# A decoder layer on one core: softplus moved from VectorE to ScalarE and GpSimd, and identity products put into TensorE's queue

## The chip, the cores and the metric

The kernel runs on one core of a Trainium2 chip. The metric is the device time of one execution in microseconds; lower is better. A core has TensorE (matmul, called PE in the profile, its weight loads PEld), VectorE (DVE), ScalarE (ACT), GpSimd (POOL) and SyncE (SP), which work in parallel; each takes its instructions in order, and they wait for each other by semaphores.

## The reference

The input is 8 rows of 256 tokens with 256 features, in float32. Three parts follow each other, each with a residual and a layer norm:

```
x = layernorm(x + mamba(x))              # per row
x = layernorm(x + cross_attention(x, ctx))   # per row, with a feed-forward of 1024
x = layernorm(x + experts(x))            # 160 experts, 8 per token, and one shared
```

The part that the change touches is the step size of the mamba block, with 512 inner channels and 16 states:

```
delta = softplus(dt @ dt_w + dt_b)       # [256 tokens, 512 channels] per row
h[t]  = h[t-1] * exp(delta[t] * A) + (delta[t] * u[t]) * B[t]
y[t]  = h[t] @ C[t]
```

Softplus of v is max(v, 0) + ln(1 + exp(-|v|)), with a correction for the rounding of 1 + exp(-|v|).

## The kernel before

Channels and features lie on the 128 partitions, tokens along the free side. The program has two stages.

**The rows.** Each of the 8 rows goes through a scan of 16 steps (n = 0 to 15), each for 32 channels times 16 states. A step has a product g on GpSimd (`product`, L527), four decays on ScalarE (`decays`, L535), two scans on VectorE (`scans`, L543) and one multiplication h on VectorE (`read_out`, L551); every fourth step TensorE adds four h (`summed`, L557 and L563) and one step later VectorE gates them (`gated`, L569). Beside the scan of row b run the head of row b+1 (`head`: projection, convolution, softplus, gate), the rest of row b-1 (`rest`: out projection po, attention, feed-forward, routing) and the scatters of rows done before (`scatter`, indirect DMAs on GpSimd, L855).

The order of every engine's instructions but SyncE's is written out by hand. `head`, `rest` and the lists are generators that say `yield place, kind`; `go_on` counts places, three per scan step, and puts out all that is due. So the softplus of the next row, at places 22 to 30 of `head`, stands at steps 7 to 10 of the scan, and its instructions stand in the queues between those of the scan.

The softplus in `head`: `with_bias` (ScalarE) writes v, then |v| into e; `exp_of` makes e = exp(-|v|) and delta = 1 + e (both ScalarE, L427 and L428); `rounding` makes e = (delta - 1) - e on VectorE (L432); `log_of` makes delta = ln(delta) on ScalarE between two table loads (L437); GpSimd subtracts e (L339); `step_sizes` makes delta = max(v, 0) + delta on VectorE (L442); `spread_out` multiplies by u on GpSimd (L446) and writes both to DRAM, from where they come back spread over the partitions for the next row. Row 0's own head (`first_head`) has the same steps in another form.

**The experts.** When the scan ends, the tokens go to the experts in turns of 128 pairs: `turn_x` transposes the pairs on TensorE (L1299) and VectorE copies them (L1301), `inner` (L1312) and `outer` (L1325) multiply by an expert's weights, `store` scatters the result. The first 56 turns, kind "a", are the list made before the last row is routed (`first_list`); the rest of the last two rows runs between them, so many places per turn (`between`). The turns "b" and "few" take what is left, after the routing of the last row. Then the eight results of each token are added and normed.

**TensorE's identity products.** `warm(n)` in the kernel before multiplies the identity by ones n times into `states`, and stands only in `first_head` (L456). Results are not used. PSUM banks for the rest come from a pool of two (`bank`), those of the turns from one of two per tag; a bank is handed out again when its last reader is done. `turned` (L206) transposes four blocks on TensorE and is called four times per row, for x1, the attention's probabilities, x2 and x3; in the profile they are pt_x from xn, pt_prob, pt_x from cn and pt_x from x.

Of the kernel before, what the change touches and what calls it, by code (L numbers as in the profile page):

```python
# [9 lines left out]
F32 = mybir.dt.float32  # L10
AF = mybir.ActivationFunctionType
# [3 lines left out]
P = 128  # L15
B, S, D = 8, 256, 256
KD = D // P
TT = S // P
DI = 512
KI = DI // P  # L20
# [57 lines left out]
def decoder_layer(  # L78
# [20 lines left out]
    nc = tc.nc  # L99
# [8 lines left out]
    ident = keep.tile([P, P], F32, name="ident")  # L108
# [28 lines left out]
    minus_one = keep.tile([P, 1], F32, name="minus_one")  # L137
    nc.vector.memset(minus_one, -1.0)

    turn = keep.tile([P, 2, -(-MOST // P)], I32, name="turn")  # L140
# [5 lines left out]
    ones = keep.tile([P, P], F32, name="ones")  # L146
# [6 lines left out]
    def bank(name):  # L153
        return pools["ps"].tile([P, NT], F32, tag="ps", name=name)
# [3 lines left out]
    def tables(name):  # L158

        if in_act[0] != name:  # L160
            nc.scalar.preload_act_table_set(name)  # L161
        in_act[0] = name
# [7 lines left out]
    def moments(src, name):  # L170

        n = src.shape[1]
        st = small.tile([P, n, 6], F32, tag="st", name=f"st_{name}")
        mv = small.tile([P, n, 2], F32, tag="mv", name=f"mv_{name}")
        for c in range(n):
            nc.vector.bn_stats(st[:, c, :], src[:, c, :])  # L176
        for c in range(n):
            nc.vector.bn_aggr(mv[:, c, :], st[:, c, :])  # L178
        return mv
# [18 lines left out]
    def layernorm(dst, src, name):  # L198
        normed(dst, src, moments(src, name), name)

    def turned(src, name):

        pt = bank(f"pt_{name}").rearrange("p (k t) -> p k t", k=KD)
        for k in range(KD):
            for c in range(TT):
                nc.tensor.transpose(pt[:, k, c * P : (c + 1) * P], src[:, c, k * P : (k + 1) * P], ident)  # L206
        return pt
# [6 lines left out]
    with ExitStack() as first:  # L214
# [3 lines left out]
        m2 = scan.enter_context(tc.tile_pool(name="m2", bufs=2, side="right"))  # L218
# [70 lines left out]
        states = held.tile([P, NG, S], F32, name="states")  # L289
# [9 lines left out]
        def head(b, made):  # L299

            t = made["t"] = {}

            def bank(name):
                return ps_head.tile([P, NT], F32, tag="ps_head", name=name)

            for j in range(KI // 2):
                if j:
                    yield 7, 1
                t["pj", j] = projected(bank, b, in_x, j, "pj")
                yield 7 * j + 2, 0  # L310
                tap_now(b, j, t)
                for e in range(2):
                    yield 7 * j + 3 + e, 0
                    taps_before(b, j, e, t)
            yield 12, 0
            tables(silus)
            nc.scalar.activation(t["u"], t["u"], AF.Silu)

            gate_silu(rows_made[b - 1])
            exps()  # L320
            yield 14, 1
            t["px"] = steps_b_c(bank, b, t)
            yield 16, 0
            b_c(b, t, made)
            for j in range(KI // 2):
                yield 17 + 3 * j, 1
                pd = wider(bank, b, j, t)
                yield 19 + 3 * j, 0
                for i in range(2):
                    with_bias(b, 2 * j + i, pd[:, i, :], t)  # L330
            nc.scalar.activation(t["e"], t["v"], AF.Abs)
            yield 23, 0
            part = slice(0, KI)
            exp_of(part, t)
            yield 24, 0
            rounding(part, t, nc.vector)
            log_of(part, t)
            yield 27, 0
            nc.gpsimd.tensor_sub(t["delta"], t["delta"], t["e"])  # L339
            yield 29, 0  # L340
            step_sizes(part, t)
            yield 30, 0
            spread_out(b, part, t, made, nc.gpsimd)
            for j in range(KI // 2):
                yield 32 + 3 * j, 1
                pz = projected(bank, b, in_z, j, "pz")
                yield 34 + 3 * j, 0
                gate_part(b, j, pz, t)
            if b + 1 < B:
                load_x(b + 1)  # L350
            made["sz"] = made["to gate"] = t["sz"]
            if b == B - 1:
                tables(silus)
                gate_silu(made)
                exps()

        def gate_silu(made):
            sz = made.pop("to gate", None)
            if sz is not None:
                nc.scalar.activation(sz, sz, AF.Silu)  # L360
# [27 lines left out]
                )  # L388

        def gate_part(b, j, pz, t):  # L390
            if j == 0:
                t["sz"] = m2.tile([P, KI, S], F32, tag="sz", name=f"sz_{b}")
            nc.scalar.copy(t["sz"][:, 2 * j : 2 * j + 2, :], pz)

# [31 lines left out]
        def exp_of(part, t):  # L426
            nc.scalar.activation(t["e"][:, part], t["e"][:, part], AF.Exp, scale=-1.0)  # L427
            nc.scalar.activation(t["delta"][:, part], t["e"][:, part], AF.Identity, bias=ones[:, 0:1])  # L428

        def rounding(part, t, eng):  # L430
            e = t["e"][:, part]
            eng.scalar_tensor_tensor(e, t["delta"][:, part], 1.0, e, ALU.subtract, ALU.subtract)  # L432
# [7 lines left out]
        def step_sizes(part, t):  # L440
            delta = t["delta"][:, part]
            nc.vector.scalar_tensor_tensor(delta, t["v"][:, part], 0.0, delta, ALU.max, ALU.add)  # L442
# [7 lines left out]
            made.setdefault("spread", [])  # L450
            made.update(u=t["u"], spread_d=t["spread_d"], spread_to=part.stop)

        def warm(n):

            for _ in range(n):
                nc.tensor.matmul(states[:, 0, :P], ident, ones, start=True, stop=True)  # L456

        def first_head(made):

            t = made["t"] = {}  # L460
            warm(10)
            for j in range(KI // 2):
                t["pj", j] = projected(bank, 0, in_x, j, "pj")
            tables(silus)
            for j in range(KI // 2):
                tap_now(0, j, t)
                for e in range(2):
                    taps_before(0, j, e, t)
                u = t["u"][:, 2 * j : 2 * j + 2]
                nc.scalar.activation(u, u, AF.Silu)  # L470
                warm(8)
            exps()
            t["px"] = steps_b_c(bank, 0, t)
            b_c(0, t, made)
            warm(4)
            for j in range(KI // 2):
                t["pd", j] = wider(bank, 0, j, t)
            for part, eng in ((slice(0, 1), nc.vector), (slice(1, KI), nc.gpsimd)):
                for k in range(part.start, part.stop):
                    with_bias(0, k, t["pd", k // 2][:, k % 2, :], t)  # L480
                nc.scalar.activation(t["e"][:, part], t["v"][:, part], AF.Abs)
                exp_of(part, t)
                rounding(part, t, nc.vector)
                log_of(part, t)
                eng.tensor_sub(t["delta"][:, part], t["delta"][:, part], t["e"][:, part])
                step_sizes(part, t)
                spread_out(0, part, t, made, eng)
                yield
# [92 lines left out]
        def rest(b, sz, xn, ct, cn):  # L581
# [20 lines left out]


            yield 0, 1
            po = bank(f"po_{b}").rearrange("p (c d) -> p c d", c=TT)
            for c in range(TT):
                for k in range(KI):
                    nc.tensor.matmul(  # L608
                        po[:, c, :], sz[:, k, c * P : (c + 1) * P], out_sb[:, k, :],
                        start=(k == 0), stop=(k == KI - 1),  # L610
# [23 lines left out]
            pt = turned(x1, f"x1_{b}")  # L634
# [36 lines left out]
            pt = turned(prob, f"prob_{b}")  # L671
# [5 lines left out]
            for m in range(KD):  # L677
                for c in range(TT):
                    nc.tensor.matmul(
                        pat[:, m, :], val[:, c, m * P : (m + 1) * P], prob_t[:, c, :],  # L680
                        start=(c == 0), stop=(c == TT - 1),
# [22 lines left out]
            pt = turned(x2, f"x2_{b}")  # L704
# [11 lines left out]
            for j in range(KF // 2):  # L716
# [4 lines left out]
                for i in range(2):  # L721
                    f = 2 * j + i
                    for k in range(KD):
                        nc.tensor.matmul(  # L724
                            ph[:, i, :], w1_sb[:, k, f * P : (f + 1) * P], x2t[:, k, :],
                            start=(k == 0), stop=(k == KD - 1),
                        )
                yield at_place + 2, 0
                for i in range(2):
                    f = 2 * j + i  # L730
# [31 lines left out]
            pt = turned(x3, f"x3_{b}")  # L762
# [362 lines left out]
        with tc.manual_schedule(engines={E_.PE, E_.Activation, E_.DVE, E_.Pool}):  # L1125
# [168 lines left out]
            def turn_x(turn):  # L1294
                t = under[turn]
                name = f"{turn[0]}_{turn[1]}"
                pt = bp.tile([P, NT], F32, tag="bt", name=f"bt_{name}")[:, : KD * P]
                for k in range(KD):
                    nc.tensor.transpose(pt[:, k * P : (k + 1) * P], t["x"][:, k * P : (k + 1) * P], ident)  # L1299
                t["xt"] = bx.tile([P, KD * P], F32, tag="bx", name=f"bx_{name}")  # L1300
                nc.vector.tensor_copy(t["xt"], pt)  # L1301
                t["pair"] = bo.tile([P, 1], I32, tag="pair", name=f"pair_{name}")
                nc.vector.tensor_tensor(t["pair"], t["x"][:, D : D + 1].bitcast(I32), t["skip"], ALU.add)
# [172 lines left out]
    with tc.If(more > 1):  # L1476
        with (
# [16 lines left out]
            for i in range(NTT):  # L1494
# [8 lines left out]
                e, late = (rest8.tile([P, TOPK], F32, tag=x, name=f"{x}_c{i}") for x in ("e", "late"))  # L1503
# [97 lines left out]
```

## Time and profile before

| | |
|---|---|
| median of 3 runs | 1321.04 us (1315.04 to 1332.0) |
| the profiled execution | 1321.17 us, span 1319.4 us |
| busy: PE, DVE, ACT, POOL | 67%, 66%, 52%, 54% of the span |
| granted TensorE clock, mean | 0.802 |
| scan of the rows | to about 805 us |
| first list ("a") | about 815 to 1037 us |
| turns "b" and "few" | about 1037 to 1258 us |
| sums of the results | to the end |

Times in the profile are microseconds from the start of the span, unless marked ns. A line of the timeline gives start, length, engine, line of the kernel, operation, result and operands, shape, and in brackets how long the engine stood idle before it and for whom. The table by stretches gives, behind from:to and length, the busy time of each engine with the number of its instructions in brackets, the granted clock as a share of full speed, and the share of time in which the DMA engines moved data with their rate. A float32 product on TensorE has two records.

### The profile page before, as it was taken

To read this page: it belongs to the slowest core of one execution; us is meant where nothing else is said; L and a number is where in the kernel's file an instruction comes from. 1 tells how busy PE (TensorE), PEld (TensorE's weight loads), DVE (VectorE), ACT (ScalarE), POOL (GpSimd) and SP (SyncE) were. 2 spreads that over 40 slices of the span, in tenths; PEclk is the share of its full clock that TensorE was granted. 3 is DMA by queue.
4 is the path that set the end of the run, shared out by engine and by line. 5 is a ranking of instruction groups with operands and counts; after the bars stand their busy time and mean duration, and the time that the engine had idled before them with its cause. 6 is when DMAs were issued, how large, how long until landed. Compare 5 with 4: busy or idle time off the path is not lost. (4 is left out here: it accounts for less than half of the span.)

```text
span 1319.4 us, 17997 instructions
## 1 busy us (share of the span) xinstructions
PE 889.7 (67%) x4670; PEld 665.9 (50%) x4670; DVE 865.8 (66%) x1606; ACT 680.8 (52%) x1545; POOL 706.8 (54%) x563
## 2 busy tenths in 40 slices
PE   6344566766865865865865756667566799788855
PEld 4222335554644644644644535545454677577643
DVE  3487679789789789789788885122245455345355
ACT  4555486686686686586687653483531211111134
POOL 0643556376686586586585844425455554445410
PEclk7576757878877878877877977789686999889889
DMA  7458668544353353354353335433654878888776
GB/s 253 128 161 209 172 175 226 158 152 119 95 164 113 94 164 113 93 163 113 94 164 94 107 104 176 149 128 109 195 176 138 269 245 275 253 269 260 242 310 280
DMA packets 182995, 227.68 MB, mean 173 GB/s; under 512 B 25126, under 2 KB 150981, under 8 KB 180836
## 3 DMA queue, kind: packets, MB, share of 16 engines
q1 hardware_dynamic: 122162, 148.47, 36.4%
q10 hardware_dynamic: 46802, 44.25, 11.9%
q0 software_dynamic: 13920, 33.72, 7.0%
q8 instruction: 40, 0.66, 0.2%
q14 instruction: 71, 0.58, 0.2%
HBM read 155.53 MB, written 74.35 MB: 174 GB/s over the span
## 5 line engine op out<-in xcount | busy, mean ns | idle before, releaser
L527 POOL TENSOR_TENSOR g<-bc,spread_du 128x1024 f32<-128x1024 f32 x128 | 301.1, 2357 | 188.0 <-DVE states L543 107.8
L535 ACT ACTIVATE decay<-spread_delta,na 128x255 f32<-128x255 f32 x512 | 243.2, 476 | 211.9 <-DVE states L543 157.1
L543 DVE TENSOR_TENSOR_SCAN states<-decay,g 128x512 f32<-128x512 f32 x256 | 313.8, 1226 | 47.6 <-ACT decay L535 23.7
L551 DVE TENSOR_TENSOR h<-states,bc 128x1024 f32<-128x1024 f32 x128 | 156.3, 1221 | 4.9 <-PE ya L563 0.3
L855 POOL DMA_INDIRECT pairs_d<-rows,placei x128 | 126.5, 988 | 47.4 <-issue 30.8
L1342 POOL DMA_INDIRECT y_d<-bo_b,pair_b x88 | 86.4, 981 | 86.8 <-DVE bo_b L1338 72.0
L161 ACT ACT_TABLE_LOAD x79 | 101.4, 1283 | 13.7 <-DMA xg<-pairs_d 9.6
L1338 DVE TENSOR_SCALAR bo_b<-by_b,xg 128x256 f32<-128x256 f32 x88 | 42.5, 483 | 80.0 <-PE by_b L1325 53.3
L1301 DVE COPY bx_a<-bt_a 128x256 f32<-128x256 f32 x56 | 23.4, 419 | 102.3 <-PE bt_a L1299 60.8
L1318 ACT ACTIVATE bg_b<-bh_b 128x128 f32<-128x128 f32 x88 | 24.4, 277 | 127.5 <-PE bt_b L1299 26.2
L1342 POOL DMA_INDIRECT y_d<-bo_a,pair_a x56 | 55.1, 983 | 59.2 <-ACT bo_a L1336 27.6
L608 PE MATMUL po<-out_sb,sz 128*128 128x256 f32 x128 | 47.8, 539 | 52.6 <-DVE sz L569 40.8
L724 PE MATMUL ph<-x2t,w_sb 128*128 128x256 f32 x256 | 70.6, 425 | 10.0 <-ACT x2t L708 5.6
L563 PE MATMUL ya<-h,over 128*32 128x256 f32 x1024 | 70.3, 406 | 9.5 <-DVE h L551 9.5
L1325 PE MATMUL by_b<-we,bg_b 128*128 128x256 f32 x176 | 61.1, 432 | 13.9 <-issue 5.0
L1312 PE MATMUL bh_a<-bx_a,we 128*128 128x128 f32 x224 | 44.9, 334 | 34.6 <-DVE bx_a L1301 22.4
L724 PEld LDWEIGHTS ph<-x2t,w_sb 128*128 128x128 f32 x256 | 55.3, 221 | 21.9 <-ACT x2t L708 7.1
L608 PEld LDWEIGHTS po<-out_sb,sz 128*128 128x128 f32 x128 | 32.8, 267 | 66.6 <-DVE sz L569 44.8
L738 PE MATMUL pf<-w_sb,ht 128*128 128x256 f32 x256 | 60.2, 390 | 7.0 <-ACT ht L731 6.9
L1312 PE MATMUL bh_b<-bx_b,we 128*128 128x128 f32 x352 | 61.0, 302 | 0.2
L385 DVE SCALAR_TENSOR_TENSOR u<-pj,cv,u 128x253 f32<-128x253 f32 (+2 forms) x96 | 45.7, 478 | 23.0 <-ACT u L376 20.8
L1318 ACT ACTIVATE bg_a<-bh_a 128x128 f32<-128x128 f32 x56 | 15.3, 277 | 84.9 <-PE bh_a L1312 42.2
(322 smaller groups left out, 1993.6 us busy)
## 6 DMA issues: line engine op xcount, KB each, us to landing
we<-in_experts_dram SPq DMA_DIRECT2D x144, 256.0 KB
pairs_d<-no_pair ACTq DMA_DIRECT2D x16, 1290.0 KB
xg<-pairs_d ACTq DMA_DIRECT2D x144, 129.0 KB
shared_w<-in_experts_dram SPq DMA_DIRECT2D x72, 256.0 KB
spread_delta<-spread_d SPq DMA_DIRECT2D x256, 64.0 KB
spread_du<-spread_d SPq DMA_DIRECT2D x256, 64.0 KB
rows<-x SPq DMA_DIRECT2D x16, 1024.0 KB
y<-y_d SPq DMA_DIRECT2D x16, 1024.0 KB
```

The source lines that it names most:

```text
L161: nc.scalar.preload_act_table_set(name)
L527: nc.gpsimd.tensor_mul(g, made["bc"][0], mid(made["spread"][n // 2][1][:, n % 2, :], NG))
L535: nc.scalar.activation(decay[j][:, e, 1:], delta[:, n % 2, 1:], AF.Exp, scale=na[:, n * NG + g : n * NG + g + 1],)
L543: nc.vector.tensor_tensor_scan(states_f[:, part], decay[j].rearrange("p g t -> p (g t)"), made[n][:, part], 0.0, ALU.mult, ALU.add,)
L551: nc.vector.tensor_mul(h, states, made["bc"][1])
L563: nc.tensor.matmul(ya[q * CH : (q + 1) * CH, k % 2, :], over, hs[q][:, g, :], start=False, stop=(g == NG - 1), skip_group_check=True, tile ...
L608: nc.tensor.matmul(po[:, c, :], sz[:, k, c * P : (c + 1) * P], out_sb[:, k, :], start=(k == 0), stop=(k == KI - 1),)
L724: nc.tensor.matmul(ph[:, i, :], w1_sb[:, k, f * P : (f + 1) * P], x2t[:, k, :], start=(k == 0), stop=(k == KD - 1),)
L855: nc.gpsimd.indirect_dma_start(out=pair_views[(b * TT + c) * TOPK + j], out_offset=bass.IndirectOffsetOnAxis(ap=placei[:, c, j : j + 1], a ...
L1312: nc.tensor.matmul(ph[:, q * n : (q + 1) * n], w[:, k * P : (k + 1) * P], t["xt"][:, k * P + q * n : k * P + (q + 1) * n], start=(k == 0), ...
L1325: nc.tensor.matmul(py, t["g"], t["w"][0][:, KD * P :], start=True, stop=True)
L1342: nc.gpsimd.indirect_dma_start(out=y_views[turn[1] + {"a": 0, "b": FIRST, "c": FIRST + MOST, "few": FIRST + MOST + OVER}[turn[0]]], out_of ...
```

## The change

Two things change.

In `head`, softplus no longer has an instruction on VectorE. ScalarE makes delta - 1 (an Identity with bias -1 into sz, the tile that later takes the gate) and max(v, 0) (a Relu in place); GpSimd makes e = (delta - 1) - e, v = max(v, 0) - e, and adds v to ln(1 + exp(-|v|)). So VectorE has two instructions less per row, ScalarE two more, GpSimd two more; `rounding` and `step_sizes` stay for row 0. The subtraction on GpSimd comes at place 26 and the addition at 28, where the subtraction was at 27 and the addition at 29.

`warm` moves out and gets the place to write as an argument, and is called at three more places, each time with the bank that the following instructions will fill: 15 products in `turned`, 40 before po in `rest`, 6 before the transposes of each turn "a". Over the run that is 480, 320 and 336 products more than the 30 in `first_head`.

```diff
+    def warm(n, to):
+        for _ in range(n):
+            nc.tensor.matmul(to[:, :P], ident, ones, start=True, stop=True)
+
     def turned(src, name):
-        pt = bank(f"pt_{name}").rearrange("p (k t) -> p k t", k=KD)
+        pt = bank(f"pt_{name}")
+        warm(15, pt)
+        pt = pt.rearrange("p (k t) -> p k t", k=KD)
...
             exp_of(part, t)
+            t["sz"] = m2.tile([P, KI, S], F32, tag="sz", name=f"sz_{b}")
+            nc.scalar.activation(t["sz"], t["delta"], AF.Identity, bias=minus_one)
             yield 24, 0
-            rounding(part, t, nc.vector)
+            nc.gpsimd.tensor_sub(t["e"], t["sz"], t["e"])
+            nc.scalar.activation(t["v"], t["v"], AF.Relu)
             log_of(part, t)
-            yield 27, 0
-            nc.gpsimd.tensor_sub(t["delta"], t["delta"], t["e"])
-            yield 29, 0
-            step_sizes(part, t)
+            yield 26, 0
+            nc.gpsimd.tensor_sub(t["v"], t["v"], t["e"])
+            yield 28, 0
+            nc.gpsimd.tensor_add(t["delta"], t["v"], t["delta"])
...
         def gate_part(b, j, pz, t):
-            if j == 0:
+            if "sz" not in t:
...
-            po = bank(f"po_{b}").rearrange("p (c d) -> p c d", c=TT)
+            po = bank(f"po_{b}")
+            warm(40, po)
+            po = po.rearrange("p (c d) -> p c d", c=TT)
...
                 pt = bp.tile([P, NT], F32, tag="bt", name=f"bt_{name}")[:, : KD * P]
+                if turn[0] == "a":
+                    warm(6, pt)
```

More of the change, by code (lines that the diff above doesn't have):

```diff
@@ L451, in spread_out @@
             made.update(u=t["u"], spread_d=t["spread_d"], spread_to=part.stop)
-        def warm(n):
-            for _ in range(n):
-                nc.tensor.matmul(states[:, 0, :P], ident, ones, start=True, stop=True)
         def first_head(made):
             t = made["t"] = {}
-            warm(10)
+            warm(10, states[:, 0, :])
             for j in range(KI // 2):
@@ L470, in first_head @@
                 nc.scalar.activation(u, u, AF.Silu)
-                warm(8)
+                warm(8, states[:, 0, :])
             exps()
@@ L474, in first_head @@
             b_c(0, t, made)
-            warm(4)
+            warm(4, states[:, 0, :])
             for j in range(KI // 2):
```

## The prediction

> **What bounds the kernel now.** I read the page first (busy shares, forty slices, chain), then the busy time by stretches, then the timelines of VectorE, ScalarE, GpSimd and TensorE in one row, then those of the expert stage. The page's chain of waits covers only the last 50 us (loads of y, 3%), which the change leaves alone, so it decides nothing here. The stretches do. First one steady row of the scan (98 us), the part of it with the softplus, and three stretches of the first list of experts:
>
> ```profile
> core 0: us, PE busy (x) PEld busy (x) DVE busy (x) ACT busy (x) POOL busy (x), PEclk, DMA share, GB/s
> 421.70:519.70 98.00, 67.76 (x351) 49.27 (x350) 85.07 (x118) 68.62 (x154) 68.21 (x48) 0.81 0.40 124
> ...
> 458.90:484.60 25.70, 13.40 (x74) 8.97 (x72) 22.42 (x25) 23.31 (x54) 22.04 (x15) 0.83 0.36 114
> ...
> 815.00:977.00 162.00, 108.99 (x508) 89.69 (x508) 44.49 (x170) 82.10 (x176) 74.38 (x84) 0.79 0.52 166
> 977.00:1013.00 36.00, 18.04 (x57) 12.80 (x56) 15.41 (x68) 4.70 (x16) 23.62 (x24) 0.56 0.42 136
> 1013.00:1037.00 24.00, 19.71 (x114) 15.40 (x112) 13.60 (x61) 6.34 (x20) 13.58 (x16) 0.95 0.64 196
> ```
>
> A row is VectorE's: 85 of 98 us. But in the 25.7 us with the softplus, ScalarE is as full (23.3), and GpSimd nearly so. In the first list nothing is full except TensorE between 1013 and 1037, with 4 us idle in 24. The granted clock is about 0.8 in most stretches, so TensorE runs at half speed some 40% of the time.
>
> VectorE, then ScalarE, in the softplus of that row:
>
> ```profile
> 471.05 4.00 DVE L432 SCALAR_TENSOR_TENSOR e<-delta,e 128x1024 f32<-128x1024 f32 x1 [2.50 <-ACT delta L428]
> ...
> 482.60 1.94 DVE L442 SCALAR_TENSOR_TENSOR delta<-v,delta 128x1024 f32<-128x1024 f32 x1
> ```
> ```profile
> 469.87 1.15 ACT L428 ACTIVATE delta<-e,ones 128x1024 f32<-128x1024 f32 x1
> ...
> 475.09 1.06 ACT L437 ACTIVATE delta<-delta 128x1024 f32<-128x1024 f32 x1 [1.17 <-DVE e L432]
> 476.17 1.28 ACT L161 ACT_TABLE_LOAD   x1
> 477.46 0.99 ACT L535 ACTIVATE decay<-spread_delta,na 128x255 f32<-128x255 f32 x2
> ```
>
> VectorE loses 2.50 + 4.00 + 1.94 us to it; ScalarE has one wait of 1.17 us and otherwise goes from one instruction to the next.
>
> TensorE: the identity products that are there already, and the places where new ones go:
>
> ```profile
> 1.63 4.08 PE L456 MATMUL states<-ones,ident 128*128 128x128 f32 x20 [1.63 <-POOL ident masks.py:199]
> ...
> 10.52 3.73 PE L456 MATMUL states<-ones,ident 128*128 128x128 f32 x32
> ...
> 149.47 1.56 PE L608 MATMUL po<-out_sb,sz 128*128 128x256 f32 x6
> 153.66 2.42 PE L608 MATMUL po<-out_sb,sz 128*128 128x256 f32 x10 [2.63 <-DVE sz L569]
> ...
> 430.04 4.64 PE L608 MATMUL po<-out_sb,sz 128*128 128x256 f32 x10 [7.74 <-DVE sz L569]
> ...
> 457.61 0.66 PE L206 MATMUL pt_x<-ident,xn 128*128 128x128 f32 x4
> ...
> 807.24 3.72 PE L608 MATMUL po<-out_sb,sz 128*128 128x256 f32 x16 [1.16 <-ACT ht L731]
> ```
>
> Two records are one product, so the first ten took 0.41 us each and the later sixteen 0.23. I take 0.22 at full clock and 0.43 at half: 8.8 us for 40, 3.3 for 15, 1.3 for 6. The place before po is idle for 7.74 us in the row at 430, for 2.63 at 153, and not at all at 807; that before pt_x of xn is never idle.
>
> **The softplus, part by part.** Seven times (the head of row 0 keeps its own form). VectorE loses 2813 ns (L432), 1848 ns (L442) and 2.5 us of wait: 7.2 us a row, 50 us in all. ScalarE gains an Identity with a bias (1147 ns, the row of L428) and a Relu over 1024 columns (1057 ns, the row of the Abs at L331): 2.2 us. GpSimd runs three operations of 2357 ns (row of L339) where it ran one: 4.7 us more.
>
> Here a rule has to be weighed. The Trainium skill, "ScalarE: Activation LUTs", section "Rules for kernel authors", puts relu, max and add on VectorE and not on ScalarE; "GPSIMD Engine Reference", "Engine selection", calls GpSimd about twice as slow for two-input operations. The rows agree only halfway. While GpSimd works, VectorE's two operations last 4.00 and 1.94 us, not the 1.2 us that h takes for the same size, so moving them is cheaper than the second rule makes it: by the rows 4.66 us leave VectorE, by the rule's ratio 2.36. But the first one speaks to what counts: ScalarE is the full engine here, and gets the work.
>
> Followed in order: L428 ends at 471.0; the new Identity takes it to 472.2, the two biased copies and the decay pair to 473.9, the Relu to 474.9, table load 476.2, Ln 477.2 (no longer waiting for VectorE), table load 478.5, decays 479.5, against 478.5 before. The scan that needs them started at 479.8 anyway. So nothing of L432 and its wait is gained: the scan is then held by ScalarE. What is gained is L442: the next scans start at 482.6 and 483.9 instead of 484.5 and 485.8. That is 1.8 us a row, for six rows 11. GpSimd's first subtraction waits for the new Identity (472.2) with g of step 12 queued behind it, wanted only at 492.4. The Identity writes sz eleven places sooner than before; the po that read this buffer last ended at 434.5. On GpSimd, delta times u ends 3.5 us later (490.5 for 487.0), and its write and the loads behind it on SP as much; the next row's first product was made at 497.7 for a scan at 517, so that is covered. Only between rows 0 and 1 VectorE stood 7.5 us behind that transfer; there it costs 1.3. Softplus together: -9.5 us. Without the ScalarE bound it would be -50, with a delay of the decays that shows in full +1 a row.
>
> **The identity products in the rows.** Before po: in the rows from 322 on, TensorE is free from 420.4 to 430.0, and 8.8 us fit. The three po products that ran ahead now come after (1.35 us), but all eight then run at full clock, and po ends at 432.8, not 434.5. VectorE waited 0.99 us there: -1.0 for five rows. In row 1 they start at 149.5, end at 158.3, and po ends at 161.9 where VectorE came at 157.3 without waiting: +4.6. Row 2 starts at 231.7 with 5 us free: +3. Before xn's transposes: 3.3 us with no gap, which moves pf and pd; VectorE took pf 2.8 us after its end, ScalarE the second pd 1.3 us: +0.5 a row, 3 in all. Those before pt_prob (3.72 us idle), cn (5.26) and x (1.78, with 2 us to spare behind it) are covered. Rows: -5 + 4.6 + 3 + 3 = +6, with the softplus -4. If the covers fail, each 15 costs 3.3 us.
>
> **The last row and the first list.** The last po has no gap: +8.8, and GpSimd's memset of xg waits for it (9.26 us), so the scatters queued behind it and the chain start later. From 815 to 977 there are 36 turns of six (47 us) and five of fifteen (16.5): 63.5 us in a stretch where TensorE idles 55. The manual order makes it one queue with the chain of the last row, and a product delays what follows it unless the next wait is for something that TensorE did not cause. Waits like 14.0 us at 931 (behind GpSimd's scatters) absorb; those on ScalarE within psc, prob and pat mostly move along. I take half of the idle time (27). A steadier clock saves something: of about 40 us of work at half clock perhaps 12. That gives +24; bounds: 0 if all idle time absorbs, 51 if none. From 977 to 1013 GpSimd issues scatters without a gap; 7 turns (9 us) lie inside 18 us of idle: 0. From 1013 to 1037 14 turns add 18 against 4 idle: +14. The stage after is paced by 250 GB/s of expert weights and is only shifted.
>
> The Trainium skill, "TensorE: Matmul & The Clock Gate", Part 1, says the clock falls to half after an idle window of about 3.4 us and returns after as long a busy one. The rows' alternation agrees (0.50 granted in the po at 430, behind 7.7 idle). By the rule the idle fill buys up to half of every slow product; by the trace those slow products are mostly not what an engine waits for, which is why I count 12 us and not more.
>
> **Sum.** -4 + 8.8 + 24 + 14 = +43. The profiled execution took 1321.17 us (span 1319.4), the median of the runs is 1321.04: 1364 us.
>
> **Rivals.** (a) Main: products in dense stretches delay the chain; 1364, range 1340 to 1392. Chance 0.55. (b) Idle time and the full clock absorb nearly everything in the first list: -4 + 0 + 0 + 9, about 1326, within 2% (1305 to 1347). For it: 55 us idle before 977, clock 0.79. Against: the dense runs at 1013 to 1037. 0.25. (c) Faster: VectorE is the bound throughout, its 50 us come off and the products hide: about 1275. It needs ScalarE to take in 2.2 us between 459 and 485, where 2.4 are free, in the gaps that VectorE made; it decides from 30 us gained in the scan. 0.05. (d) Nothing absorbs, and ScalarE's longer stretch delays decays by 2 us a row: -4 + 12 + 9 + 51 + 18 is 1407. 0.15. That the products do not run, or not at these places, is ruled out by the instruction order of the changed kernel: 1136 of them.
>
> Two per cent (1294.6 to 1347.5) is what a measurement of this kernel can tell from no change. Faster 0.05, same 0.26, slower 0.69. Leaving out about a tenth on each side, the lower half of (b) with (c), the upper of (d): 1314 to 1400.
>
> **What would show it.** Row length about 96 us, with VectorE waiting on decays where the rounding stood; ScalarE without the 1.17 us wait; the row at 140 to 165 longer by about 5; po after 810 later by 9; the turns between 1013 and 1037 taking 38 us instead of 24, and TensorE's clock above 0.9. It is wrong if rows shrink by over 4 us, or if the end of the first list moves by less than 20 us against the end of the scan.

## The result and the profile after

The changed kernel takes 1374.16 us (median of 4 runs, 1371.45 to 1378.67), the kernel before 1324.75 beside it: ratio 1.0396, 95% interval 1.0357 to 1.0435. It is slower, by about as much as forecast (1364 us). The profiled execution has a span of 1369.7 us against 1319.4, 50.3 more, and a mean granted clock of 0.896 against 0.802.

The busy time by stretches of the changed kernel, first a steady row of the scan, then the three parts of the first list (columns as before: length, busy time of each engine with its instructions, granted clock, DMA share, GB/s):

```profile
core 0: us, PE busy (x) PEld busy (x) DVE busy (x) ACT busy (x) POOL busy (x), PEclk, DMA share, GB/s
...
437.70:533.20 95.50, 82.89 (x552) 66.67 (x551) 78.68 (x116) 70.89 (x157) 71.95 (x50) 0.95 0.44 128
832.60:1016.30 183.70, 155.54 (x1043) 141.93 (x1044) 44.69 (x163) 81.86 (x174) 74.93 (x85) 0.93 0.44 140
1016.30:1057.50 41.20, 27.94 (x177) 25.94 (x176) 16.92 (x75) 5.52 (x18) 24.51 (x25) 0.79 0.40 125
1057.50:1089.80 32.30, 32.30 (x264) 31.37 (x263) 14.72 (x61) 6.46 (x19) 13.04 (x16) 1.00 0.53 150
```

The row is shorter than the 98.0 us before, and VectorE is busy in it for 6.4 us less. The list is where the time went: in its last part TensorE is busy for 32.30 of 32.30 us, at full clock, with identity products among the real ones.

The softplus in that row, on ScalarE and then on VectorE (start, length, engine, line, operation; in brackets the idle time before it):

```profile
485.20 1.15 ACT L439 ACTIVATE delta<-e,ones 128x1024 f32<-128x1024 f32 x1
486.38 1.15 ACT L344 ACTIVATE sz<-delta,minus_one 128x1024 f32<-128x1024 f32 x1
...
489.07 1.04 ACT L347 ACTIVATE v<-v 128x1024 f32<-128x1024 f32 x1
...
491.42 1.06 ACT L448 ACTIVATE delta<-delta 128x1024 f32<-128x1024 f32 x1
```
```profile
489.17 1.23 DVE L549 TENSOR_TENSOR_SCAN states<-decay,g 128x512 f32<-128x512 f32 x1 [2.93 <-ACT decay L541]
...
494.81 1.23 DVE L549 TENSOR_TENSOR_SCAN states<-decay,g 128x512 f32<-128x512 f32 x1 [2.36 <-ACT decay L541]
```

ScalarE goes through its longer list without a wait, and VectorE stands where its rounding used to be, waiting for decays. The scans of the whole run, before and after (count, busy time and mean ns of one, idle time ahead of them and for whom):

```profile
L543 DVE TENSOR_TENSOR_SCAN states<-decay,g 128x512 f32<-128x512 f32 x256 | 313.8, 1226 | 47.6 <-ACT decay L535 23.7 <-POOL g L527 7.5 <-DVE h L551 0.5
```
```profile
L549 DVE TENSOR_TENSOR_SCAN states<-decay,g 128x512 f32<-128x512 f32 x256 | 313.8, 1226 | 95.2 <-ACT decay L541 68.8 <-POOL g L533 10.5 <-DVE h L557 0.5
```

The wait for decays grew from 23.7 to 68.8 us: of the 50 us that left VectorE (33 of work and 17 of waiting, by the prediction's figures), 45 came back as waiting for ScalarE.

The forty products before po, in row 1 and in the last row on TensorE, and the instruction that takes po on VectorE in row 1, after and then before:

```profile
151.27 9.20 PE L204 MATMUL po<-ones,ident 128*128 128x128 f32 x80
160.30 3.62 PE L616 MATMUL po<-out_sb,sz 128*128 128x256 f32 x16
...
816.38 9.20 PE L204 MATMUL po<-ones,ident 128*128 128x128 f32 x80 [1.16 <-ACT ht L739]
825.42 3.62 PE L616 MATMUL po<-out_sb,sz 128*128 128x256 f32 x16
```
```profile
163.96 0.69 DVE L621 TENSOR_TENSOR xn<-xn,po 128x512 f32<-128x512 f32 x1 [4.15 <-PE po L616]
```
```profile
157.26 0.68 DVE L613 TENSOR_TENSOR xn<-xn,po 128x512 f32<-128x512 f32 x1
```

From the starts of the last h, of the first and last turn "a" and of the total of the last row's routing in both traces, the 50.3 us divide so (the first turn and that total on TensorE are shown, before and then after): the scan ends 9.2 later (802.9 to 812.0); from there to the first turn 8.2 more; from the first turn to that total (975.45 and 1016.25) 23.4 more; to the last turn "a" 14.6 more; the stage after it 7.3 less; the end 2.2 more.

```profile
815.23 0.66 PE L1299 MATMUL bt_a<-ident,xg 128*128 128x128 f32 x2 [4.28 <-issue]
...
975.45 0.43 PE L899 MATMUL total_b<-so_far,ones 128*128 128x160 f32 x2
```
```profile
832.64 0.41 PE L1309 MATMUL bt_a<-ident,xg 128*128 128x128 f32 x2 [2.26 <-POOL xg L1236]
...
1016.25 0.43 PE L907 MATMUL total_b<-so_far,ones 128*128 128x160 f32 x2
```

The scan is not what was forecast: it should have been 4 us shorter. So the experiments ask what the softplus is worth, part by part and row by row.

### The profile page after: what moved, and what is told of

Its sections match the earlier page's. It is cut to its first block, busy times and chain, and to the rows that moved or that the text cites. A ratio compares the mean times of both kernels' runs of the same rounds, so it can differ in the third digit from the quotient of the medians.

```text
span 1369.7 us, 22507 instructions
## 1 busy us (share of the span) xinstructions
PE 1069.7 (78%) x6942; PEld 878.1 (64%) x6942; DVE 833.3 (61%) x1592; ACT 695.0 (51%) x1559; POOL 735.2 (54%) x577
## 5 line engine op out<-in xcount | busy, mean ns | idle before, releaser
L549 DVE TENSOR_TENSOR_SCAN states<-decay,g 128x512 f32<-128x512 f32 x256 | 313.8, 1226 | 95.2 <-ACT decay L541 68.8
L1311 DVE COPY bx_a<-bt_a 128x256 f32<-128x256 f32 x56 | 23.7, 423 | 158.8 <-PE bt_a L1309 101.0
L161 ACT ACT_TABLE_LOAD x79 | 101.4, 1283 | 23.2 <-DMA xg<-pairs_d 19.2
L204 PEld LDWEIGHTS bt_a<-ones,ident 128*128 128x128 f32 x672 | 89.1, 202 | 11.2 <-issue 7.9
L204 PE MATMUL bt_a<-ones,ident 128*128 128x128 f32 x672 | 90.3, 286 | 6.6 <-issue 6.6
L204 PEld LDWEIGHTS pt_x<-ones,ident 128*128 128x128 f32 x720 | 84.8, 196 | 5.6 <-issue 3.7
L204 PE MATMUL pt_x<-ones,ident 128*128 128x128 f32 x720 | 88.0, 281 | 0.0
L204 PE MATMUL po<-ones,ident 128*128 128x128 f32 x640 | 75.2, 280 | 9.6 <-ACT ht L739 9.6
L204 PEld LDWEIGHTS po<-ones,ident 128*128 128x128 f32 x640 | 73.7, 195 | 13.3 <-ACT ht L739 12.5
L732 PE MATMUL ph<-x2t,w_sb 128*128 128x256 f32 x256 | 65.0, 399 | 12.7 <-ACT x2t L716 10.7
```

Source lines behind the costliest of these rows:

```text
L204: nc.tensor.matmul(to[:, :P], ident, ones, start=True, stop=True)
L549: nc.vector.tensor_tensor_scan(states_f[:, part], decay[j].rearrange("p g t -> p (g t)"), made[n][:, part], 0.0, ALU.mult, ALU.add,)
L732: nc.tensor.matmul(ph[:, i, :], w1_sb[:, k, f * P : (f + 1) * P], x2t[:, k, :], start=(k == 0), stop=(k == KD - 1),)
```

## The experiments

Every ratio is to runs of the kernel before on the same chip. The first four runs were on a chip where that kernel has a median of 1280.61 us, the next four on one with 1321.11, the last four there again with 1319.03. "Scan" is the time from the first h of row 0 to the last h of row 7, divided by the first h of rows 2, 3 and 7. At the end of this section a table has these for all kernels. Each row of it is one trace: three traces whose scan has the code of before (the first profile, e4 and e12) differ by 3.3 us in rows 0 and 1, 2.6 in row 2, 2.5 in rows 3 to 6 and 6.2 in the whole scan, and a smaller difference between two traces tells nothing.

**1. Each part alone.** The whole change with all but one part taken out again.

```diff
 e1: the new softplus; no warm(40, po), no warm(15, pt), no warm(6, pt)
 e2: the old softplus; warm(40, po) alone
 e3: the old softplus; warm(15, pt) alone
 e4: the old softplus; warm(6, pt) alone
```

> The new softplus without a single added identity product. Theory (the products are the loss, the softplus is a small gain that ScalarE caps): the scan ends some 9 us sooner than before, 1315 us, ratio 0.993. Rival (the scan's 9 us of loss come from ScalarE's longer stretch, since VectorE's wait for decays rose from 24 to 69 us): the scan ends later than before, 1330 us or more. A third one (VectorE is the bound, its 50 us come off): 1275 us.

Measured: 1.0026 [1.0002, 1.0050]. Not faster; a miss.

> Old softplus; only the 40 products before each po. Theory of places: five rows gain 1 us each, rows 1 and 2 lose 4.6 and 3, the last row loses 8.8 with nothing to hide it: 1333 us, ratio 1.008. Rival (idle filling and the steadier clock pay for them): 1315 us or less.

Measured: 1.0115 [1.0048, 1.0181].

> Old softplus; only the 15 products in the four transposes of every row. By my step: 0.5 us a row in the scan and five groups of 3.3 us in the chain of the last row, about 3 plus 10: 1334 us, ratio 1.010. By the trace of the changed kernel, where row 1 became 12 us longer, rather more: 1345 us. If their places are covered: 1321 us.

Measured: 1.0083 [1.0058, 1.0108].

> Old softplus; only the 6 products in each turn of the first list. The scan unchanged. Theory of places: 36 turns before the last row's routing add 47 us of which half is absorbed, the last 14 turns 14 us: 1350 us, ratio 1.024. Rival (idle time absorbs all before the routing): 14 us, 1335 us.

Measured: 1.0194 [1.0130, 1.0259].

The excesses sum to 4.2%, the whole change has 4.0%: the parts add up. The three sets of products cost about what was worked out for them. The softplus does not bring what was worked out for it. In its trace the rows 3 to 6 are shorter (389.2 us for four against 394.8 to 397.3 in the three traces with the scan of before), but rows 0 and 1 are longer by 8.3 us than in e4.

**2. The softplus by rows.** The new form only where the steps of rows 3 to 7 are made, that is in the scans of rows 2 to 6.

```diff
-            t["sz"] = ...            # new softplus for every row
+            if b > 2:                # new softplus
+                t["sz"] = ...
+            else:                    # rounding and step_sizes on VectorE, as before
```

> The new softplus for the steps of rows 3 to 7 only (made during the scans of rows 2 to 6); rows 1 and 2 keep the old one; no identity products. If what the new softplus loses is lost only in the scans of rows 0 and 1 (3.1 and 5.1 us there when all rows have it) and the later rows gain 1.1 to 2.7 us each, the scan ends about 9 us earlier than before: ratio 0.993. Rival, that the loss comes wherever the new form appears first, and moves to row 2 and 3: ratio 1.000 to 1.003, and the row from h_0 of row 2 to h_0 of row 3 longer by 3 us or more.

Measured: 0.9963 [0.9944, 0.9983]. Rows 0 and 1 are back at 183.4 us, and row 2, the first with the new form, has 97.6, within the 95.1 to 97.7 of the scan of before. The rival, that the loss moves on to the first row with the new form, wanted a ratio of 1.000 or more. So the loss belongs to the rows 0 and 1 and not to the first use. The gain of 5 us is smaller than the 9 forecast; the next two runs ask which part of the new form gains.

**3. The softplus by operations.** On the kernel before, one of the two instructions leaves VectorE and the other stays.

```diff
 e6
             rounding(part, t, nc.vector)
+            nc.scalar.activation(t["v"], t["v"], AF.Relu)
...
-            step_sizes(part, t)
+            nc.gpsimd.tensor_add(t["delta"], t["v"], t["delta"])
 e7
+            nc.scalar.activation(t["sz"], t["delta"], AF.Identity, bias=minus_one)
-            rounding(part, t, nc.vector)
+            nc.gpsimd.tensor_sub(t["e"], t["sz"], t["e"])
```

> On the kernel before, only the step sizes leave VectorE: the ramp on ScalarE ahead of the logarithm, the sum on GpSimd; the rounding stays on VectorE. The prediction puts the whole gain of a steady row (1.8 us) on this operation. By it, with one more ScalarE operation of 1.04 us instead of two, rows 2 to 6 gain 1.8 us each, and rows 0 and 1 lose about half of what they lost with both (4 us of 8): ratio 0.996. Rival, that the gain comes from the rounding, which stands ahead of the last operations of the decays: 1.000 or above.

Measured: 0.9967 [0.9948, 0.9986].

> On the kernel before, only the rounding leaves VectorE: the Identity on ScalarE, the difference on GpSimd; the step sizes stay on VectorE. The prediction gives this part nothing in a steady row, since ScalarE is full there and the Identity of 1.15 us delays the decays by as much: ratio 1.002, with the loss in rows 0 and 1 (about 4 us). Rival, that the gain of the steady rows is this part's: 0.996.

Measured: 1.0040 [1.0025, 1.0056].

The prediction's division holds: in the steady rows all of the gain is the step sizes' (386.5 us for rows 3 to 6, against 394.8 to 397.3 in three traces of the scan of before) and the rounding, though it is the longer instruction and has a wait of 2.5 us ahead of it, brings nothing when it leaves: 398.8. e7 alone would not show why, because there the step sizes that stay on VectorE suffer: they start 1.02 us late, behind GpSimd's subtraction, and last 3.35 us instead of 1.94 (L444, at 489.49). But taking the rounding away on top of the step sizes does not help either, where nothing of the softplus is left on VectorE: rows 3 to 6 have 389.2 and 389.0 us in e1 and e5, against 386.5 in e6 (and 385.9 in e9 below). In rows 0 and 1 the step sizes lose 3.6 us against e4, hardly more than two traces can tell, and the 1.2 us of the rounding are less than that.

**4. ScalarE relieved.** The new softplus, with its two ScalarE operations on GpSimd.

```diff
-            nc.scalar.activation(t["sz"], t["delta"], AF.Identity, bias=minus_one)
+            nc.gpsimd.tensor_scalar_add(t["sz"], t["delta"], -1.0)
-            nc.scalar.activation(t["v"], t["v"], AF.Relu)
+            nc.gpsimd.tensor_scalar_max(t["v"], t["v"], 0.0)
```

> The new softplus with its two ScalarE operations (Identity and ramp, 1.15 and 1.04 us) put on GpSimd, where the trace has no such one-input operation of 128x1024 (1.0 to 2.4 us each is an estimate from the 2.34 us of a two-input one there). ScalarE then has no more to do than before. If the delay of the decays on ScalarE is what rows 0 and 1 lose, they no longer lose: about 8 us better than the new softplus as it is, ratio 0.994 to 0.996. Rival, that the longer chain through GpSimd to the spread of delta (1.3 us later at GpSimd, 3 us later landed) is what they lose: no better than 1.003, and with 2 to 5 us more on GpSimd worse, up to 1.015.

Measured: 1.0184 [1.0145, 1.0223], slower than either theory had it. The groups of instructions of this run (line, operation, count, busy time and mean ns of one, idle time before):

```profile
L343 POOL TENSOR_SCALAR sz<-delta 128x1024 f32<-128x1024 f32 x7 | 19.5, 2781 | 25.1 <-ACT delta L438 19.7 <-DVE h L556 5.4
L346 POOL TENSOR_SCALAR v<-v 128x1024 f32<-128x1024 f32 x7 | 19.4, 2777 | 0.0
...
L345 POOL TENSOR_TENSOR e<-sz,e 128x1024 f32<-128x1024 f32 x7 | 16.4, 2342 | 0.0
```

The one-input operation costs more here than the two-input one. With 5.6 us more on GpSimd each steady row is longer (402.3 for four) and rows 0 and 1 most of all, by 14.2 us. This run does not tell how much of their loss is ScalarE's own delay; it tells that they are at least as sensitive to GpSimd's chain from the logarithm to the two writes of delta and delta times u.

**5. What can be kept.** The step sizes moved for the steps of rows 3 to 7 only; and the same with the fifteens in the scans of rows 2 to 6.

```diff
 e9, on the kernel before
             rounding(part, t, nc.vector)
+            if b > 2:
+                nc.scalar.activation(t["v"], t["v"], AF.Relu)
...
+            if b > 2:
+                nc.gpsimd.tensor_add(t["delta"], t["v"], t["delta"])
+            else:
+                step_sizes(part, t)
 e10, on e9: 15 products ahead of turned(x), for the tails of rows 1 to 5
```

> On the kernel before, the step sizes leave VectorE for the steps of rows 3 to 7 only; rounding and rows 1 and 2 stay as they were. With the step sizes moved in all rows, the scans of rows 2 to 6 were 12 us shorter together and those of rows 0 and 1 3.6 us longer. If the loss belongs to these two rows and not to the operation, it goes away and the gain stays: scan end 10 to 12 us earlier than before, ratio 0.991 to 0.994. Rival, that the first row with the new form always pays: 0.997, no better than with all rows.

Measured: 1308.20 us, 0.9924 [0.9896, 0.9953]; the scan is 746.3 us. Faster than both kernels, by 0.8% against the one before; the rival wanted 0.997, and row 2, the first with the new form, has 96.3 us, within the spread of before.

> The same, and 15 identity products ahead of each of the four turned tiles of the tails of rows 1 to 5, which run in the scans of rows 2 to 6; none in row 0's tail and in the last. In the run with the fifteens everywhere these scans were 7 us shorter together, that of row 1 3.2 us longer, and the list behind the scan 14 us longer. If TensorE's clock in these scans is what shortens them, this version is 4 to 7 us faster than the one without: ratio 0.987 to 0.990. My step in the prediction (0.5 us more per row, 2.5 us together) gives 0.994 to 0.996. Rival, that the difference of the scans was chance: the same as without.

Measured: 0.9931 [0.9912, 0.9950]; the scan is 746.7 us. The same row by stretches, of e9 and then of e10:

```profile
424.00:520.00 96.00, 67.74 (x350) 50.28 (x350) 83.50 (x118) 69.63 (x156) 70.59 (x49) 0.84 0.44 127
```
```profile
424.00:520.00 96.00, 76.11 (x470) 59.89 (x470) 80.74 (x117) 68.94 (x155) 69.99 (x49) 0.91 0.42 126
```

The products ran (120 records more), the clock rose from 0.84 to 0.91, and the scan did not become shorter (746.3 and 746.7 us). The 4 to 7 us that e3's rows seemed to promise did not come: here TensorE's clock is not what a row waits for. e3's shorter rows may have been chance: rows 2 to 6 have 487.9 us in e3, 490.2 in e12, 492.1 in the first profile and 495.0 in e4.

**6. The whole without its softplus, and the kernel before once more.**

```diff
 e11: the whole change, with rounding and step_sizes as before
 e12: the kernel before, unchanged
```

> The whole change but for its softplus: all identity products, and the softplus of the kernel before. If the parts add up as they did one by one (excesses of 1.15, 0.83 and 1.94% without the softplus), 1.039, and the whole change loses or gains nothing by its softplus; by the prediction's step, which gives the softplus 9.5 us, 1.047.

Measured: 1.0388 [1.0353, 1.0422], against 1.0396 [1.0357, 1.0435] with it.

> The kernel before, unchanged, for a second profile of it. Its scan ended at 802.9 us in the first profile, and at 808.0 in the run that differs from it only behind the scan; which of the two is usual decides how much of the 9.2 us by which the changed kernel's scan ends later is the change's. By the runs of single parts (additive within 2 us) about 808, with rows 1 and 2 at 92 and 97.7 us and not 90.1 and 95.1.

Measured: the scan ends at 806.3 us and is 755.6 long, row 1 has 92.0 and row 2 95.4 us. So the first profile's 802.9 is at the early end of what this code gives (808.0 in e4), and 9.2 us overstate what the change does to the end of the scan; against the later two traces it is 4.0 to 5.7.

All scans, in us:

| kernel | rows 0, 1 | row 2 | rows 3 to 6 | row 7 | scan |
|---|---|---|---|---|---|
| before | 180.2 | 95.1 | 397.0 | 82.0 | 754.3 |
| before again (e12) | 183.4 | 95.4 | 394.8 | 82.0 | 755.6 |
| sixes alone (e4; scan as before) | 183.5 | 97.7 | 397.3 | 82.0 | 760.5 |
| after | 197.4 | 97.7 | 385.2 | 84.4 | 764.6 |
| after without softplus (e11) | 189.2 | 97.5 | 392.5 | 84.4 | 763.6 |
| softplus alone (e1) | 191.8 | 96.6 | 389.2 | 81.2 | 758.8 |
| forties alone (e2) | 187.0 | 98.3 | 394.4 | 82.7 | 762.4 |
| fifteens alone (e3) | 186.4 | 94.6 | 393.3 | 82.0 | 756.3 |
| softplus from row 3 (e5) | 183.4 | 97.6 | 389.0 | 81.2 | 751.3 |
| step sizes (e6) | 187.1 | 96.4 | 386.5 | 81.2 | 751.2 |
| rounding (e7) | 184.7 | 97.1 | 398.8 | 81.6 | 762.2 |
| additions on GpSimd (e8) | 197.7 | 99.0 | 402.3 | 82.0 | 781.0 |
| step sizes from row 3 (e9) | 182.8 | 96.3 | 385.9 | 81.2 | 746.3 |
| the same and fifteens (e10) | 183.6 | 96.1 | 385.0 | 82.0 | 746.7 |

## Why the prediction was right, and the step in it that failed

The time was right (1364 us forecast, 1374 measured, within the range), and so was its main reason: rival (a), products in dense stretches delay the chain. From the end of the scan to the last turn "a" there are 46 of the 50 us, where rival (b) left 9. That the sum came within 10 us is in part luck: the scan ended some 13 us later against the first profile than forecast, 8 to 10 against the other traces of its code, and the stage after the list took 7 us less, for no known reason. By its steps:

**The softplus, -9.5: failed.** The whole change with and without its new softplus differs by 0.08% in time, within both intervals, and by 1.0 us in the scan. The six rows' gain of 1.8 us each was right in size where it was seen: rows 3 to 6 are 7.3 us shorter with it (385.2 against 392.5), and by e6, e9 and e1 its source is L442 alone, as worked out. What failed are two terms: "for six rows 11", which takes rows 1 and 2 for rows like the steady one, and "Only between rows 0 and 1 VectorE stood 7.5 us behind that transfer; there it costs 1.3". Row 2 gains nothing (97.7 against 97.5), and rows 0 and 1 lose 8.2 us. The stretches of rows 0, 1 and 3 of the whole without the softplus, and then of rows 0 and 1 with it, show how they differ:

```profile
48.80:139.70 90.90, 36.35 (x162) 19.87 (x162) 68.86 (x68) 49.84 (x89) 44.13 (x20) 0.63 0.66 167
139.70:238.00 98.30, 76.35 (x479) 58.87 (x483) 72.40 (x80) 56.05 (x116) 51.51 (x24) 0.82 0.69 180
...
335.60:433.80 98.20, 84.04 (x552) 67.65 (x551) 84.00 (x117) 68.89 (x154) 68.70 (x48) 0.95 0.42 125
```
```profile
47.40:142.30 94.90, 35.49 (x162) 19.62 (x162) 66.84 (x68) 51.96 (x92) 48.88 (x22) 0.63 0.65 163
142.30:244.80 102.50, 78.79 (x466) 60.65 (x470) 69.63 (x78) 57.89 (x118) 55.95 (x26) 0.80 0.68 174
```

In rows 0 and 1 VectorE is busy 69 of 91 and 72 of 98 us only, and the DMA engines for two thirds, against 0.42 in row 3. The prediction overlooked three things there. First, there was less to take off: the rounding (L432 of the kernel before) lasts 4.00 us from row 3 on, but 1.23 in rows 0, 1 and 2; its mean of 2813 ns is of both kinds. Second, ScalarE's longer list costs its full length all the same: VectorE's waits for decays rise from 4.6 to 10.5 us in row 0 and from 7.0 to 16.5 in row 1, and those for g in the whole run from 8.3 to 10.5. Third, fourteen of the sixteen fills of 1290 KB (`pairs_d<-no_pair`) fall into these two rows, and ScalarE issues them between its decays. In row 1, ScalarE and VectorE of e9 (where this row has the old form):

```profile
205.14 0.38 ACTq L266 DMA_DIRECT2D pairs_d<-no_pair  x1
...
227.24 0.39 ACTq L266 DMA_DIRECT2D pairs_d<-no_pair  x1
227.76 1.89 ACT L540 ACTIVATE decay<-spread_delta,na 128x255 f32<-128x255 f32 x4 [3.18 <-DMA spread_du<-spread_d]
...
228.84 2.57 DVE L548 TENSOR_TENSOR_SCAN states<-decay,g 128x512 f32<-128x512 f32 x2 [1.00 <-ACT decay L540]
```

And SyncE, ScalarE and VectorE of e6 (where the step sizes are moved):

```profile
204.55 0.38 SPq L450 DMA_DIRECT2D spread_d<-v  x1
...
209.27 0.43 ACTq L266 DMA_DIRECT2D pairs_d<-no_pair  x1
209.83 1.89 ACT L536 ACTIVATE decay<-spread_delta,na 128x255 f32<-128x255 f32 x4 [5.49 <-DMA spread_d<-v]
...
231.74 0.40 ACTq L266 DMA_DIRECT2D pairs_d<-no_pair  x1
232.34 1.89 ACT L536 ACTIVATE decay<-spread_delta,na 128x255 f32<-128x255 f32 x4 [5.70 <-DMA spread_du<-spread_d]
...
210.90 2.56 DVE L544 TENSOR_TENSOR_SCAN states<-decay,g 128x512 f32<-128x512 f32 x2 [2.89 <-ACT decay L536]
...
233.42 2.56 DVE L544 TENSOR_TENSOR_SCAN states<-decay,g 128x512 f32<-128x512 f32 x2 [3.53 <-ACT decay L536]
```

In e6 ScalarE stands 4.9 and 5.1 us ahead of these two issues (5.5 and 5.7 with the issue itself), the decays behind them come late, and VectorE waits 2.9 and 3.5 us for those; in e9 the first of the two fills goes out without a wait, the other behind one of 2.7, and VectorE waits 1.0 us. The traces keep the semaphore events, and they tell what ScalarE waits for. The DMAs of SyncE and ScalarE share eight semaphores, and each fill waits for one of them, the one that it is going to use itself, until the DMA that had it before has landed. In e6 that is the write of delta times u for the fill at 209.27 (`spread_d<-v`, issued at 204.55, landed at 209.25), and a load of the spread delta times u for the one at 231.74 (landed at 231.72). For the fill at 205.14 in e9 it is a load of bc, landed at 196.22 already. So a fill, which has no need of the next row's step sizes, waits for their transfer, and all that ScalarE has behind it waits too; when GpSimd delivers later, the fill goes out later. In e8 one fill stands 11.7 us behind `spread_d<-v`. Over all sixteen fills ScalarE stands 10.3 to 15.1 us in the ten traces in which rows 1 and 2 have their step sizes from VectorE, 21.4 in e6, 22.9 in e1, 23.2 in the whole change and 34.4 in e8.

In the whole change the DMA engines also stand still for longer before delta is there. The DMA's busy tenths and rates in the 1 us slices from 190 to 230 us, of the whole without the new softplus and then with it:

```profile
DMA  6758999995000499981947999999991445999999
GB/s 193 176 186 275 366 299 215 184 155 175 14 0 0 157 352 343 258 200 61 334 155 240 306 319 371 155 289 245 166 238 44 119 138 191 379 312 226 185 137 141
```
```profile
DMA  6965999997200000089999950289999999912454
GB/s 128 266 187 144 314 350 323 255 247 150 64 0 0 0 0 0 0 285 350 285 282 276 214 164 6 61 299 272 379 363 181 276 182 156 286 46 74 137 150 135
```

Two empty slices became six, in a stretch in which the slices around them are full: what was to be moved then comes later. That the loss is these two rows' is shown by e5 and e9, and what holds a fill's issue is shown by the semaphores. How the 8.2 us divide between ScalarE's longer list, the waits for g and the fills is not shown: a run without the fills, or with them on another queue, was not made.

**ScalarE as the cap of the steady rows: held.** Its instructions came in the order and lengths worked out, the wait before ln was gone, VectorE waited 2.93 us on decays where the rounding stood, the row took 95.5 us where 96 were expected. The rule weighed there, that relu and add belong on VectorE and not on ScalarE (the Trainium skill, "ScalarE: Activation LUTs", "Rules for kernel authors"), is half right here: with the Identity on ScalarE the kernel is slower (e7, 1.0040), with the ramp of the step sizes there it is faster (e9, 0.9924), since VectorE is the busier engine over the row and ScalarE has the 1.04 us.

**Identity products in the rows, +6: held in sum.** Without the new softplus the scan is 763.6 us, against 754.3, 755.6 and 760.5: +3 to +9. In row 1 VectorE waited 4.15 us for po (+4.6 forecast), in row 2 1.94 (3). The 1.0 us that the forties were to save in each later row, and the fifteens' +0.5 a row, are less than these traces can tell (394.4 us for rows 3 to 6 in e2; e10).

**The last po, +8.8:** 8.2. **The first part of the list, +24:** 23.4. **977 to 1013, 0:** +2.9; six turns lie there, not the seven of the prediction. **1013 to 1037, +14:** +11.7, from 20.6 to 32.3 us between the starts of the first and the last of these fourteen turns. The half that I took as absorbed was a guess between bounds of 0 and 51, and that it fell right is luck; nor is it even. By the runs of single parts, on the chip of e1 to e4, the 16.5 us of fifteens there cost 14.0 (149.1 us from the first turn to the last row's total, against 135.1 in e1) and the 47 us of sixes only 15.3 (150.4). That the fifteens stand within the chain of the last row and the sixes mostly beside it fits this, but was not tested apart; nor was how much of it is idle time filled and how much the steadier clock, for which 12 us were taken.

**The stage after, 0:** 7.3 us shorter, which I can't assign to the change: between the first and the last of the turns "b" there are 216.6 and 216.5 us in the two profiles of before, and 207.9 to 220.4 in the others, in no order.

The clock rule that I weighed (the Trainium skill, "TensorE: Matmul & The Clock Gate", Part 1) agrees in its direction: with the idle time filled, the granted clock rose to 0.95 in the rows and 0.93 in the list; its window of about 3.4 us no run here tests. Counting little for it was right in the rows (e10). Rival (c), VectorE's 50 us off, falls with the 45 us of new waits on decays.

## What to carry to other kernels

Before an instruction is moved off the busiest engine, follow the engine that gets it through that very stretch: here the longer of two instructions brought nothing (its cover was ScalarE's own chain) and the shorter one brought 2 us a row. And follow it in the first rows apart from the steady ones; here the rounding was shorter there and ScalarE had DMA issues between its decays, and the move was worth making in five rows and not in the two before. A DMA issue in an engine's queue is part of that engine's chain: look which transfer it waits for before you make that transfer later. Filling TensorE's idle time raised its clock (0.84 to 0.91 in e10) and brought nothing where no engine waited for TensorE, and it cost nearly its full length where the products stood in the chain (8.2 of 9.2 us at the last po).

## What had not been expected of the hardware

- GpSimd's operation with one input and a constant, 128x1024 in float32, took 2781 ns (2777 for the maximum), its operation with two inputs 2342 to 2359 ns. The Trainium skill, "GPSIMD Engine Reference", section "Engine selection", has one-input operations at roughly line rate and only two-input ones slow; the measurement decides: here the one with one input takes longer. For two inputs the page agrees, with 2.34 us against the 1.22 of VectorE's h.
- VectorE's rounding (128x1024, two inputs from SBUF) lasted 1.23 us in row 1 of e9, where GpSimd stood idle beside it, and 4.00 us in the steady row of the first profile, where GpSimd worked. What GpSimd does beside an instruction of VectorE is part of what moving that instruction is worth.
- The two chips give the scan about the same length (760.5 us in e4 on the one, 755.6 in e12 on the other, and 754.3 in the first profile), but the stretch from the first turn to the last row's total took 135.1 us on the first (e1) and 158.2 on the second (e12), with the same code there. What makes it was not looked for; it is why times are compared on one chip only.
